# Group 0's block products piled up in PSUM, and a second group wholly on two levels, in a routed low-rank FFN kernel

## The chip, the cores and the metric

The kernel runs on one core of a Trainium2 chip. A core has a matrix engine (TensorE, PE in the profile, with its weight loads as PEld), a vector engine (VectorE, DVE), a scalar engine (ScalarE, ACT), GpSimd (POOL) and SyncE (SP), which here only issues DMAs. They run side by side and meet at semaphores. Matmuls write to PSUM, eight banks of 128 x 512 f32; the rest lives in SBUF. The metric is the device time of one execution in microseconds; lower is better. The kernel before takes 790.79 us, median of three runs (790.68 to 791.86).

## What is computed

All is f32. There are 64 samples of 64 channels and 1024 features, 4096 rows in all. Each sample picks one 64 x 64 matrix, which mixes its channels; the mixed rows z go through a low-rank layer of 64 adapters with rank 16, of which a router picks 16 per row; the result is added to x.

```python
W = weights[condition]                            # (64, 64, 64)
z = einsum('bct,bcd->bdt', x, W)                  # channel mix, per sample
scores = z @ Wr.T                                 # (4096, 64)
top_vals, top_idx = top_k(scores, 16)
G = zeros.at[rows, top_idx].set(softmax(top_vals))
h = einsum('nd,krd->nkr', z, A)                   # 1024 -> 64 * 16
out = einsum('nkr,kdr->nd', h * G[:, :, None], B) # 64 * 16 -> 1024
return x + 2 * out
```

The two large steps are products of 1024 x 1024 matrices (A, then B) with all rows.

## The kernel before

**Tiling.** Rows are handled in eight groups of 512. For a group, the first product ("h") is x A, 512 x 1024 by 1024 x 1024; mixing by W comes after it, since it acts on rows ("zp" matmuls, `gated`, L305), and VectorE multiplies the gates in on the way from PSUM to the tiles `hb`. The second product ("o") is `hb` times B, added to x and stored.

**Seven products instead of eight.** Each product is split into 2 x 2 quadrants and done by a Strassen-Winograd scheme: seven block products p1 to p7, called *parents*, of sums of quadrants of the left side (`left_sums`, L337: steps s1 to s4) and of the right side (`a_sums`, `b_sums`), and sums of their results. A parent on level 1 is a *whole* product: two halves of four matmuls of 512 columns. A parent on level 2 is split once more into seven *leaves* of two matmuls of 256 columns each, by the same scheme: `prepare` makes the left leaves on VectorE (tiles `l_t`), the right leaves are made once, staged in SBUF (`hs_...` for A, `os_...` for B), stored to DRAM and fetched again when used.

**The router** has 16 extra columns beside each 256 of A (272 in all, `KC`). From group 2 on the h parents carry them along, and `scores` finishes them with the channel mix. Groups 0 and 1 compute the router apart: `scores_t` (L170) multiplies x with `wr_sb`, `turn` transposes it back, and `scores` applies the mix. Then `route_top`, `exps`, `rest` (once for each of a group's four tiles), `scaled` and `gates` (transposes "gp" by TensorE, copied to `gg`) give the gates.

**Order of parents.** h of group 0, o of group 0, h of group 1, h of group 2, o of group 1, h of group 3, o of group 2, and so on. Group 0 is on level 1 throughout, and so are p1 and p2 of group 1's h; all else is on level 2. The order within a product is in `FIRST` (group 0) and `ORDER`.

**Who decides the order.** It is written out by hand. `run` (L544) issues a parent's instructions in program order for every engine, and hooks hang other work into it: `at(n, "mid" | "late" | "end", f)` runs f in the slot of parent n. Within a slot the left leaves of the next parent are prepared between "mid" and "late"; what is finished of the parent before is added up by its `done`. Each engine executes its own instructions in that order, and so does each DMA queue: nearly all DMAs are issued from SP, in order.

**Group 0's results.** Each whole parent has its own two banks. ScalarE copies them to an SBUF tile `m`, and `done` (L634 for h, L697 for o) adds such tiles to each other and to the output tiles `o`, wide adds of 128 x 1024 by VectorE.

**Leaf making.** `leaf_steps` (L392) gives for each right-hand block four VectorE steps and their stores; B's blocks without raw copies in the input also store their raw quadrants (L405, three DMAs). `a_steps` and `b_steps` are lists of such steps that hooks in group 0 work off. They stage in the pool `bsum` of four buffers, so a step waits for the store of the step that had its buffer. The leaves of A's p1 and p2 come last (staged in `zp`), in group 1's slots, since A11 and A21 are still used whole until then.

**Fetching.** `fetch` (L443) loads the next leaf in order of use into a ring of 13 buffers (`bp`); each level-2 product frees its buffer and fetches one. The first 13 fetches are hooked to the first two parents of group 1's h.

**Memory.** A's blocks stay. `bpool` holds B's blocks, `wr_sb` and helpers for group 0; `second_level` (L808) closes all of group 0's pools at once, at the start of group 1, and opens those of the second level in their room.

**The start.** x and A are loaded in the order of use from SP (the first x block from ScalarE's queue); ten warm-up matmuls run meanwhile. The row numbers `idx` for the gather of W come first on VectorE.

Of the kernel before, what the change touches and what calls it, by code (L numbers as in the profile page):

```python
# [24 lines left out]
RING = 13  # L25
# [4 lines left out]
def kernel(  # L30
# [47 lines left out]
    bpool = first_group.enter_context(tc.tile_pool(name="bpool", bufs=1, side="right"))  # L78
    mp0 = first_group.enter_context(tc.tile_pool(name="mp0", bufs=5, side="right"))
    rp0 = first_group.enter_context(tc.tile_pool(name="rp0", bufs=3, side="right"))  # L80
    bsum = first_group.enter_context(tc.tile_pool(name="bsum", bufs=4, side="right"))
# [10 lines left out]
    def load_x(g: int, i: int, j: int, queue=nc.sync):  # L92

        t = xq[g, i, j] = xp.tile([P, CH, HN], F32, tag=f"x{i}{j}", name=f"x_{g}_{i}{j}")
        queue.dma_start(t, x_t[g, i, j])
# [9 lines left out]
    load_x(0, 0, 0, nc.scalar)  # L105
    a11 = load_block("a11", a_t, 0, 0, apool, 2)
# [6 lines left out]
    wr_sb = bpool.tile([P, 2 * CH, K], F32, name="wr_sb")  # L113
# [4 lines left out]
    b11 = load_block("b11", b_t, 0, 0, bpool)  # L118
# [9 lines left out]
    for j in range(2):  # L128
        h = slice(j * C, (j + 1) * C)
        nc.vector.tensor_scalar(  # L130
            idx[h],
            cond_b[h].rearrange("p (n j) -> p n j", j=2)[:, :, j],
            float(C),
            row[h],
            ALU.mult,
            ALU.add,
        )
# [4 lines left out]
    for _ in range(10):  # L142
        nc.tensor.matmul(idle, lhsT=ident, rhs=ident, start=True, stop=True)
    two_i = bpool.tile([P, K], F32, name="two_i")
# [15 lines left out]

    gather(0)
# [8 lines left out]
    def scores_t(st):  # L170
# [14 lines left out]
        st_sb = bpool.tile([P, 2 * HN], F32, tag="st_sb", name=f"st_sb_{g}")  # L185
# [3 lines left out]
    def turn(st):  # L189
# [7 lines left out]
        zr = bpool.tile([P, TPG, K], F32, tag="zr", name=f"zr_{g}")  # L197
# [194 lines left out]
    def leaf_steps(k, j, block, pool, tag="leaf"):  # L392

        (q11, q12), (q21, q22) = quads(block, WIDTH[k])
        made = {}

        def staged(name):
            if tag == "z":
                return pool.tile([P, 2, 2 * (HALF + KC)], F32, tag=tag, name=name)[:, :, : WIDTH[k]]
            t = pool.tile([P, 2 * (HALF + KC)], F32, tag=tag, name=name)  # L400
            return t[:, : 2 * WIDTH[k]].rearrange("p (c k) -> p c k", c=2)
# [5 lines left out]
        def step(op_, p, a, b):  # L407
            def f():
                made[p] = staged(f"{k}s_{j}_{p}")
                op_(made[p], *(made[v] if isinstance(v, str) else v for v in (a, b)))  # L410
                nc.sync.dma_start(leaf_d[k, j, p], made[p])
# [3 lines left out]
        if k == "o":  # L415
# [8 lines left out]
        return [  # L424
            step(sub, "p7", q22, q12),
            lambda: sub(q12, q12, q11),
            step(sub, "p6", q22, q12),
            step(sub, "p4", q21, "p6"),
        ]


    parents, to_fetch, ring, stay = [], [], [], {}
# [10 lines left out]
    def fetch():  # L443
        if to_fetch:
            key = to_fetch.pop(0)
            t = pools["bp"].tile([P, 2 * (HALF + KC)], F32, tag="b", name="l{}_{}_{}".format(*key))
# [12 lines left out]
    pools = {"mp": mp0, "rp": rp0}  # L459

    def parent(kind, st, j, level, left, whole, done):


        g = st["g"]
        par = {"kind": kind, "g": g, "j": j, "level": level, "done": done}

        width = WIDTH[kind] if g > 1 else HALF

        def begin():
            name = f"m_{g}_{kind}_{j}"  # L470
            if g and kind == "h":
                m = pools["zp"].tile([P, 2, 2 * (HALF + KC)], F32, tag="z", name=name)
            else:
                m = pools["mp"].tile([P, 2, BANK], F32, tag="m", name=name)
            v = halves(m)[:, :, :, :width]
            par.update(m=m, v=v, q=[[v[:, i, k, :] for k in range(2)] for i in range(2)])
            par.update(bank={}, val={}, width=width)

        def whole_w(c):
            w = whole[j][:, c, :]  # L480
            return w.rearrange("p (d k) -> p d k", d=2)[:, :, :HALF] if kind == "h" else w

        def half(s):

            par["bank"][s] = acc.tile([P, BANK], F32, tag="acc", name=f"{kind}_{g}_{j}_{s}")
            for c in range(CH):
                piece(s, c)
# [499 lines left out]
```

## Time and profile before

| what | value |
|---|---|
| median of three runs | 790.79 us (790.68 to 791.86) |
| the profiled execution's own time | 790.09 us |
| its span, first to last instruction | 788.0 us |
| TensorE busy | 774.4 us, 98% of the span |
| VectorE busy | 626.8 us, 80% |
| ScalarE busy | 191.7 us, 24% |
| DMA moved | 206.82 MB, mean 262 GB/s |
| group 0's h begins on TensorE | 6.16 us |
| group 0's o begins | 61.81 us |
| group 1's h begins | 120.72 us |
| group 2's h begins | 166.37 us |
| last matmuls begin | 779.64 us |

The profile is one execution. Busy times are unions per engine; the difference between the execution's time and its span is outside the instructions. In rows of the timeline the columns are start, length, engine, line, operation, output tiles and input tiles, shape, count, and in brackets the idle time of the engine before it and what ended it. A matmul in f32 appears as two records. Names in the profile have no numbers: `h_p_x` is a bank of some parent of h, `o_p_w` of o, `hs_p_p` and `os_p_p` are staged leaves, `h_p_p` and `o_p_p` their places in DRAM, `lh_p_p` and `lo_p_p` the fetched ones, `a`, `at`, `b`, `bt` the right-hand blocks.

### The profile page before, as it was taken

Reading aid. Unit: us, or ns where it says so; the run is one execution under the profiler, and the core shown is the slowest. Engines: PE = TensorE matmul, PEld = TensorE weight load, DVE = VectorE, ACT = ScalarE, POOL = GpSimd, SP = SyncE. Lnnn points to the kernel's source line nnn. Section 1 sums busy time; section 2 is a strip of 40 time slices with the busy share of each in tenths; the row PEclk is TensorE's granted clock in tenths of the full one; section 3 lists DMA queues with packets and bytes.
Section 4 is the critical chain, followed back from the end, with each engine's and each line's share of the span. In section 5 each row is a group of like instructions: output and inputs, shape, how many; then the busy total and the mean of one; then the engine's idle time right before and its main releaser. Section 6 shows DMA issues by size and latency. Waiting matters only on the chain.

```text
span 788.0 us, 14615 instructions
## 1 busy us (share of the span) xinstructions
PE 774.4 (98%) x5348; PEld 608.9 (77%) x5348; DVE 626.8 (80%) x1297; ACT 191.7 (24%) x500; POOL 36.8 (5%) x39
## 2 busy tenths in 40 slices
PE   9999999999999999999999999999999999999996
PEld 5444445888888888887888888888888888887885
DVE  0789798878688868897788976888868887788886
ACT  1131121321222222222222222232223232222221
POOL 4100100002000020000200010000200000000000
PEclk9999999999999999999999999999999999999998
DMA  8813779955888858896788958889488894688895
GB/s 319 335 58 140 258 280 374 334 170 150 323 271 286 294 197 294 277 305 226 257 270 283 315 184 304 249 280 353 124 313 280 275 340 142 201 271 281 304 366 215
DMA packets 114454, 206.82 MB, mean 262 GB/s; under 512 B 12112, under 2 KB 32848, under 8 KB 113488
## 3 DMA queue, kind: packets, MB, share of 16 engines
q1 hardware_dynamic: 112928, 204.02, 76.1%
q0 software_dynamic: 1024, 1.05, 0.5%
q8 instruction: 43, 0.70, 0.4%
q10 hardware_dynamic: 432, 0.82, 0.3%
q14 instruction: 27, 0.22, 0.1%
HBM read 172.74 MB, written 33.11 MB: 261 GB/s over the span
## 4 chain that ended last, share of the span: by engine, by line
PE 83%; DVE 9%; DMA 6%; issue 1%; SPq 0%; ACT 0%; DVEq 0%
PE h_p_x L530 21%; PE o_p_x L530 19%; PE h_p_w L530 11%; PE o_p_w L530 10%; PE h_p_y L530 5%; PE h_p L495 5%; PE o_p_y L530 5%; PE zp L318 4%; DMA h_p_p<-hs_p_p 2%; DVE o L84 2%; DVE os_p_p L87 2%; DMA o_p_p<-os_p_p 1%; PE gp L298 1%; DMA out_dram<-o 1%; DVE hs_p_p L87 1%
## 5 line engine op out<-in xcount | busy, mean ns | idle before, releaser
L530 PE MATMUL o_p_x<-lo_p_p,l_t 128*128 128x256 f32 x584 | 143.0, 379 | 0.8 <-issue 0.8
L530 PEld LDWEIGHTS o_p_x<-lo_p_p,l_t 128*128 128x128 f32 x584 | 110.8, 190 | 16.6 <-issue 1.2
L84 DVE TENSOR_TENSOR o<-o,m_o_p 128x1024 f32<-128x1024 f32 (+1 forms) x73 | 86.0, 1196 | 1.2 <-DMA o<-in_x_dram 0.7
L84 DVE TENSOR_TENSOR m_h_p<-m_h_p,m_h_p 128x1088 f32<-128x1088 f32 (+1 forms) x56 | 70.3, 1267 | 5.5 <-ACT m_h_p L492 5.2
L84 DVE TENSOR_TENSOR m_h_p<-h_p_w,l_a 128x272 f32<-128x272 f32 (+1 forms) x47 | 20.6, 438 | 57.1 <-PE h_p_w L530 57.0
L153 POOL DMA_INDIRECT w_st<-in_cw_dram,idx x32 | 36.0, 1125 | 530.4 <-PE zp L318 513.9
L530 PE MATMUL h_p_x<-a,l_t 128*128 128x272 f32 (+1 forms) x208 | 55.9, 391 | 0.0
L530 PE MATMUL h_p_w<-lh_p_p,l_t 128*128 128x272 f32 (+1 forms) x188 | 51.2, 395 | 0.0
L530 PE MATMUL o_p_w<-lo_p_p,l_t 128*128 128x256 f32 x196 | 51.0, 383 | 0.0
L530 PE MATMUL h_p_x<-lh_p_p,l_t 128*128 128x272 f32 (+1 forms) x188 | 50.5, 391 | 0.0
L564 ACT COPY l_b<-h_p_x 128x272 f32<-128x272 f32 (+1 forms) x47 | 18.1, 385 | 118.8 <-PE h_p_x L530 118.8
L530 PEld LDWEIGHTS h_p_x<-a,l_t 128*128 128x128 f32 x208 | 39.5, 190 | 7.8
L331 DVE TENSOR_TENSOR hb<-zp,gg 128x512 f32<-128x512 f32 x64 | 39.9, 683 | 7.0 <-PE zp L318 7.0
L530 PE MATMUL h_p_x<-at,l_t 128*128 128x272 f32 (+1 forms) x168 | 45.0, 390 | 0.0
L564 ACT COPY l_b<-o_p_x 128x256 f32<-128x256 f32 x49 | 18.3, 373 | 103.7 <-PE o_p_x L530 103.7
L530 PEld LDWEIGHTS h_p_x<-lh_p_p,l_t 128*128 128x128 f32 x188 | 35.7, 190 | 6.9
L530 PEld LDWEIGHTS o_p_w<-lo_p_p,l_t 128*128 128x128 f32 x196 | 36.6, 190 | 5.1
L530 PEld LDWEIGHTS h_p_w<-lh_p_p,l_t 128*128 128x128 f32 x188 | 35.0, 191 | 6.5
L84 DVE TENSOR_TENSOR m_o_p<-o_p_w,l_a 128x256 f32<-128x256 f32 x48 | 20.3, 423 | 24.3 <-PE o_p_w L530 24.3
L318 PEld LDWEIGHTS zp<-w_st,m_h_p 64*64 64x64 f32 x2048 | 31.7, 135 | 7.8 <-issue 6.9
L530 PEld LDWEIGHTS h_p_x<-at,l_t 128*128 128x128 f32 x168 | 31.9, 190 | 6.3
L318 PE MATMUL zp<-w_st,m_h_p 64*64 64x64 f32 x2048 | 34.3, 220 | 0.3 <-issue 0.3
(148 smaller groups left out, 1342.6 us busy)
## 6 DMA issues: line engine op xcount, KB each, us to landing
lo_p_p<-o_p_p SPq DMA_DIRECT2D x280, 256.0 KB
lh_p_p<-h_p_p SPq DMA_DIRECT2D x141, 272.0 KB
o<-in_x_dram SPq DMA_DIRECT2D x32, 512.0 KB
lo_p_p<-in_b_t_dram SPq DMA_DIRECT2D x63, 256.0 KB
x<-in_x_t_dram SPq DMA_DIRECT2D x31, 512.0 KB
out_dram<-o SPq DMA_DIRECT2D x31, 512.0 KB
o_p_p<-os_p_p SPq DMA_DIRECT2D x28, 256.0 KB
h_p_p<-hs_p_p SPq DMA_DIRECT2D x21, 272.0 KB
```

Source lines behind the costliest of these rows:

```text
L84: nc.vector.tensor_tensor(o, a, b, ALU.add)
L87: nc.vector.tensor_tensor(o, a, b, ALU.subtract)
L153: nc.gpsimd.indirect_dma_start(out=w_st[:, i, :], out_offset=None, in_=cw, in_offset=bass.IndirectOffsetOnAxis(ap=idx[:, n : n + 1], axis=0),)
L298: nc.tensor.transpose(gp[:, i, :], st["g2"][i].rearrange("p a k -> p (a k)"), ident)
L318: nc.tensor.matmul(zp[b][e * D : (e + 1) * D, c, s, :], lhsT=halves(z)[r, s, c // 2, ds(c % 2 * P + e * D, D)], rhs=ws[g][r, 2 * i + s, :] ...
L331: nc.vector.tensor_tensor(tokens(hb[j, i])[:, :, :, b, :], zp[b], g_ij[:, :, :, b, :], ALU.mult)
L495: nc.tensor.matmul(par["bank"][s], lhsT=left()[j][:, c, ts(s, P)], rhs=whole_w(c), start=c == 0, stop=c == CH - 1, skip_group_check=True,)
L530: nc.tensor.matmul(bank, lhsT=v[:, c, :], rhs=w[:, c, :width], start=first and c == 0, stop=c == 1, skip_group_check=True,)
L564: nc.scalar.copy(par["val"][n], par["bank"]["x"])
```

## The change

**Whole products pile up.** In group 0 the parents of one product no longer have banks of their own. Three pairs of banks, X, Y and W, take them in turn, and a parent that belongs to a sum is accumulated on what its pair holds. For h the pair X takes p1, then p6, p7 and p4 on top; W takes p5 and then p3; Y takes p2. ScalarE copies X where a partial sum is itself needed (after p1, p6, p7 and p4 for h, after p1, p6 and p5 for o); VectorE adds the other pairs from PSUM, one bank at a time (`add_piled`).

**Group 1.** All its h parents are on level 2 and carry the router's columns, as in the later groups. Its `scores_t` and `turn` go; its scores, routing, gates and `gated` move into the slots of group 2's h, in a schedule that the last group shares with one slot's difference. In the last group the fourth `rest`, `scaled` and `gates` each come a place earlier.

**Leaves.** A's p1 and p2 leaves are made at the very start, before all sums, by four steps each. As A11 and A21 are still needed whole, the partial difference goes to a tile apart, and ScalarE copies it into the block later. Their six stores are issued on ScalarE's queue. The index computation and group 0's gather come after the first four of these steps, group 0's x sums before `a_sums(1)`. B's leaves come in another order and partly earlier, A's others too; `b_sums(4)` is one slot earlier.

**Pools.** Blocks that are done with early (`b11`, `bt3`, `wr_sb` and helpers) go to `epool`, closed after o's fifth parent; there the first six ring buffers (`bp0`) and the pools for left leaves and copies are opened, and the first six fetches are hooked to the slot of o's sixth parent. The rest of the pools is closed and reopened at group 1, as before.

**Loads.** The first x block comes in two parts, A11 in four; there are seven warm-up matmuls. The output tiles' input quarters are loaded in the order (0,0), (1,1), (1,0), (0,1), in the last group at o's parents -2, -1, 1 and 2.

```diff
-RING = 13
+RING, RING0 = 13, 6
...
-    load_x(0, 0, 0, nc.scalar)
-    a11 = load_block("a11", a_t, 0, 0, apool, 2)
+    load_x(0, 0, 0, nc.scalar, 2)
+    a11 = load_block("a11", a_t, 0, 0, apool, 4)
...
-    for _ in range(10):
+    for _ in range(7):
         nc.tensor.matmul(idle, lhsT=ident, rhs=ident, start=True, stop=True)
...
-    def leaf_steps(k, j, block, pool, tag="leaf"):
+    def leaf_steps(k, j, block, apart=None):
...
+        queue = nc.sync if apart is None else nc.scalar
...
-                nc.sync.dma_start(leaf_d[k, j, p], made[p])
+                queue.dma_start(leaf_d[k, j, p], made[p])
...
+        t1 = q12 if apart is None else apart.rearrange("p (c k) -> p c k", c=2)
+        steps = [
             step(sub, "p7", q22, q12),
-            lambda: sub(q12, q12, q11),
-            step(sub, "p6", q22, q12),
+            lambda: sub(t1, q12, q11),
+            step(sub, "p6", q22, t1),
             step(sub, "p4", q21, "p6"),
         ]
+        return steps if apart is None else steps + [lambda: nc.scalar.copy(q12, t1)]
...
+            pool = pools["bp0" if fetched[0] % RING < RING0 else "bp1"]
...
-        width = WIDTH[kind] if g > 1 else HALF
+        width = WIDTH[kind]
...
+    PILES = {
+        "h": dict(p1="X", p2="Y", p5="W", p6="x", p7="x", p4="x", p3="w"),
+        "o": dict(p1="X", p7="W", p6="x", p2="Y", p5="x", p4="w", p3="x"),
+    }
+
+    def whole_parent(kind, st, j, left, whole, piles, done, copied=None):
+        n = PILES[kind][j].lower()
...
+        def piece(s, c):
...
+            nc.tensor.matmul(
+                piles[n, s],
+                lhsT=left()[j][:, c, ts(s, P)],
+                rhs=w,
+                start=c == 0 and PILES[kind][j].isupper(),
+                stop=c == CH - 1,
+                skip_group_check=True,
+            )
...
+    def add_piled(o, piles, n):
+        for s in range(2):
+            add(o[:, s, :], o[:, s, :], piles[n, s])
...
-        f for j in ("p2", "p1", "p3", "p5", "p6", "p7", "p4") for f in leaf_steps("o", j, br[j], bsum)
+        f for j in ("p1", "p2", "p7", "p3", "p5", "p6", "p4") for f in leaf_steps("o", j, br[j])
...
+    def second_level():
+        open_pools(early, ("lp", 2), ("lt", 2), ("bp0", RING0), side="right")
+
+    def steady():
+        open_pools(first_group, ("mp", 3), ("zp", 6), ("bp1", RING - RING0), ("rp", 4))
...
+    steps_of(first_steps["p1"], 4)
+    rows_to_gather()
+    gather(0)
+    steps_of(first_steps["p2"], 4)
     x_operands(st)
+    sums(st, "x_sums", "s1_s2")
     a_sums(1)
-    sums(st, "x_sums", "s1_s2")
     a_sums(2)
...
-    at(o + 4, "mid", b_sums, 4)
...
+    at(o + 3, "end", b_sums, 4)
+    for k, lst, n in (
+        (h + 2, b_steps, 4),
+        (h + 3, b_steps, 4),
+        (h + 5, a_steps, 4),
+        (h + 6, a_steps, 5),
+        (o, a_steps, 2),
+        (o + 1, b_steps, 5),
+        (o + 1, a_steps, 1),
+        (o + 2, a_steps, 6),
+        (o + 3, a_steps, 2),
+        (o + 4, b_steps, 7),
+        (o + 5, b_steps, 7),
+    ):
+        at(k, "end", steps_of, lst, n)
+    at(o + 6, "mid", steps_of, b_steps, 2)
     at(o + 6, "end", steps_of, b_steps, 99)
...
-    at(o + 2, "mid", scores_t, nxt)
-    at(o + 3, "mid", turn, nxt)
...
+    at(o + 4, "end", second_level)
+    at(o + 5, "mid", fetches, 3)
+    at(o + 5, "end", fetches, 3)
+    h = sts[1]["h"]
+    at(h + 0, "mid", fetches, 4)
+    at(h + 0, "end", fetches, 3)
...
+    for st in sts[1:]:
+        n, g = st["h"] + 7, st["g"]
+        near = g in (1, NG - 1)
...
+        if near:
+            slots = ((2, "end"), (3, "late"), (3, "end"), (4, "late"))
...
+        at(n + (4 if near else 8), "end" if near else "mid", scaled, st)
+        at(n + (5 if near else 8), "mid" if near else "late", gates, st)
```

## The prediction

> **What bounds the kernel now.** I read the page's busy shares first, then TensorE's list of waits, then the timelines of TensorE, VectorE and SP over the first 180 us (where the change lies), and busy time by stretches for the DMA rate.
>
> ```profile
> PE 774.4 (98%) x5348; PEld 608.9 (77%) x5348; DVE 626.8 (80%) x1297; ACT 191.7 (24%) x500; POOL 36.8 (5%) x39
> ...
> PE idle L143 <- POOL ident masks.py:199: 1.5, 1, 1.5
> PE gp L298 <- ACT g L286: 1.4, 1, 1.4
> ...
> PE o_p L495 <- DVE b L87: 0.8, 1, 0.8
> PE h_p_w L530 <- DVE m_h_p L84: 0.5, 1, 0.5
> PE o_p L495 <- DVE hb L87: 0.4, 1, 0.4
> ```
> TensorE works 774.4 of 788.0 us. Less TensorE work shortens the span one for one, every new TensorE wait lengthens it one for one, and removing waits can give only the few us listed. VectorE counts where it makes TensorE late.
>
> ```profile
> 20.34 3.67 PE L177 MATMUL st<-x,wr_sb 128*64 128x256 f32 x32
> 23.94 3.70 PE L495 MATMUL h_p<-a,sum_p 128*128 128x512 f32 x8
> ...
> 120.72 13.90 PE L495 MATMUL h_p<-a,x 128*128 128x512 f32 x32
> 134.45 1.03 PE L530 MATMUL h_p_x<-at,x 128*128 128x256 f32 x4
> ...
> 140.49 1.03 PE L530 MATMUL h_p_x<-at,l_t 128*128 128x256 f32 x4
> ```
> Differences of starts are the true costs, since matmuls overlap: 3.60 us for the router's scores, 13.73 for two whole products, 6.04 for a two-level product of 256 columns (seven leaves). One of 272 columns takes 6.41 (chain of waits, 287.40 to 293.81).
>
> ```profile
> 0.00:5.00 5.00, 3.47 (x16) 3.47 (x17) 0.29 (x2) 1.28 (x1) 0.77 (x7) 1.00 0.61 206
> 5.00:10.00 5.00, 4.60 (x15) 2.39 (x15) 0.44 (x2) 0.00 (x0) 0.00 (x0) 1.00 0.84 297
> 10.00:20.00 10.00, 10.00 (x24) 4.10 (x22) 1.27 (x3) 1.76 (x3) 7.54 (x8) 1.00 1.05 390
> ...
> 120.00:130.00 10.00, 10.00 (x25) 4.42 (x24) 7.95 (x24) 1.66 (x3) 0.00 (x0) 1.00 1.07 399
> ```
> The last two columns are DMA share and GB/s: DMA is full from 10 us on, and again at 120 to 130. It is the second resource without slack.
>
> ```profile
> 18.99 2.43 DVE L87 TENSOR_TENSOR a<-a,a 128x2176 f32<-128x2176 f32 x1 [8.70 <-DMA a<-in_a_t_dram]
> ...
> 85.09 1.42 DVE L87 TENSOR_TENSOR os_p_p<-b,os_p_p 128x512 f32<-128x512 f32 x2 [4.47 <-DMA h_p_p<-hs_p_p]
> ...
> 122.40 0.69 DVE L87 TENSOR_TENSOR os_p_p<-b 128x512 f32<-128x512 f32 x1 [1.55 <-DMA o_p_p<-os_p_p]
> ...
> 129.89 0.42 DVE L84 TENSOR_TENSOR l_t<-x 128x256 f32<-128x256 f32 x1
> ...
> 74.98 1.84 SPq L95 DMA_DIRECT2D x<-in_x_t_dram  x4
> ```
> Leaves are staged in four buffers, so VectorE stops until a store four leaves back has landed (the waits at 85.09 and 122.40), and what is queued behind the leaf stops too. Group 1's first left-hand leaves (`l_t`) come at 129.89; they are needed only after two whole products, from 134.45.
>
> **TensorE's work.** Group 1: before 13.73 + 5 x 6.04 = 43.93; after 7 x 6.41 = 44.87: +0.94. Its `scores_t` goes: -3.61 (83.38 to 86.99). `turn`: -0.84 (93.96 to 94.80). Its scores become 32 small matmuls, 1.07 us (694.63 in the chain), instead of 16 in 0.61: +0.46. Group 0 issues the same matmuls. Sum -3.05.
>
> **Waits that go.** `b_sums(4)` is a slot earlier: -0.76. The hidden sums wait (0.41): between the product and the next stand the same zp and one subtraction, but fewer adds lie ahead on VectorE: -0.41. The wait at 142.88 belonged to late A leaves, which are now made first: -0.50. The last group's fourth `rest` moves ahead of about 2.7 us of adds (716.74 to 719.46), its gate transposes do not move on TensorE: -1.42. Sum -3.1; with the work, -6.1.
>
> **The adds.** Piles take some 7 us of adds from VectorE in group 0, at 1.2 us each (74.46 row: 1.22). Adding a bank pair from PSUM is two 128x512 operations, by the row `hb<-zp` 0.64 each, so as dear as one wide add. The copies by ScalarE fall too. All of this is beside TensorE: 0, unless VectorE binds.
>
> **The start.** x and A11 in smaller parts let the first product begin near 4.6 instead of 6.16 (seven warm-up pairs at 4.23/10 us end at 4.5). But the second needs A21. Bytes ahead of it: 3.31 MB; the windows give 2.52 MB by 10 us, then 390 GB/s: 12.0, plus about 1.2 to land, and the trace begins that product at 13.30. Gain 0 (bounds -0.3 to +0.5).
> The eight A-leaf subtractions (8 x 0.73 = 5.9 us) lie in VectorE's idle 10.3 to 19; without that cover they would cost their length. Group 0's gather goes behind four of them, to about 13: four issues (3.8 us) and 9.1 to landing make 26, before the scores at 32. ScalarE's queue now has six stores that wait for VectorE ahead of its first copy; the copy is not due until the next pile write, after 30.
> The stores are not free. They are 6 x 0.279 = 1.67 MB, 4.1 us at 404 GB/s (20 to 30 us), put among the loads. By the same sum A12 is complete at 17.6 and seen by VectorE at 18.99, so the router's weights (5.73 MB) land near 19.7, only just before `st` at 20.34. Shares: the first x block (ScalarE's queue) and half of A11 (SP's), alike in size and pieces, landed at 6.12 and 5.94, so equal shares; that puts all stores ahead of the weights: +4.1. The Trainium skill (DMA: Bandwidth & Descriptors, Queues, rings and completion order) says an engine takes turns between queues by packets; against loads in pieces of 8704 bytes, stores in 2176 get less than half and about four fifths of them come before the weights: 3.3. `st` then starts 2.7 to 3.5 late: **+3.1** (bounds 0 to 4.1). What follows (`p5`, `p6`) has its sums by then.
>
> **The entry to group 1.** Two whole products used to cover it; now the third leaf product of its first parent needs `t2`, 1.8 us in. Group 1 starts at 120.72 - 5.06 (scores, turn, sw) - 1.17 + 3.1 = 117.6, so `t2` is due at 119.4. VectorE's order puts the four `l_t` behind `os_p4_p5`, whose buffer is that of `os_p6_p5`.
> (1) Group 0's o starts at 64.9; its second zp block ends 9.4 later, as before (61.81, 71.22): 74.3. hb, sum, two A7 steps (1.29 + 1.22 + 0.72 + 0.72): 78.2. Group 1's x loads go out behind that store.
> (2) From x issue to the landing of the first store behind it took 10.1 (74.98 to 85.09). Now three raw copies and a leaf lie there, 0.77 MB more: 2.2. VectorE, out of buffers, resumes at 78.6 + 12.3 = 90.9.
> (3) Up to the first output store: two leaves 1.43, `o` 1.3, sum 1.2, A4 2.9, A3 1.45, `o` 1.2, sum 1.15, b21 2.25, A3 1.45, `o` 1.3 = 15.6: 106.5. Product p4, which needs b21 (103.8), is due at 103.7: no matter.
> (4) From that store to `os_p6_p5`: nine leaves and six raw copies of 0.262 MB, three fetches of 0.279, two stores and a load of 0.524: 6.34 MB in one queue, in order. At 399 GB/s 15.9 us; at 364 (stretches with many raw copies) 17.4. First data 1.2 after issue, landing 0.5 after the last: 124.1 to 125.6.
> (5) `os_p4_p5` 0.70, t1 and t2 0.8: 125.6 to 127.1, against 119.4. TensorE waits 6.2 to 7.7: **+7.0** (bounds 3, x loads at the rate of other loads, to 8.5). Next late would be the following parent's `l_t`; they come with their product. SP's fetches for it, issued behind the same stores, land some 3 us ahead of use.
>
> **Edits with one answer.** The last group's input quarters are loaded in another order and later on SP: each still has a product (6 us) before its add, against 4.55 for such a load (113.05); 0, and without that cover the add waits, not TensorE. The ring's split, the pools' sides and the earlier B leaves issue what was issued before; six A-leaf stores leave SP's queue at 135 to 146, where six fetches for group 1's first two products take their room. New waits on reused memory concern stores of a product or more earlier: 0.
>
> **The clock.** The trace's warm-up matmuls take 0.21 us each and the same shape at 49.94 takes 0.11: half rate after the idle start. No later idle stretch here passes 1.5 us, so the rows alone price a long wait at its length. The Trainium skill (TensorE: Matmul & The Clock Gate, Part 1) lets the array fall to half rate after an idle window of about 3.4 us and stay for as long: 3.4/2 = 1.7 more for the 7 us wait, nothing for 3.1. With the rule the sum has +1.7; I take it.
>
> **Sum.** -6.1 + 3.1 + 7.0 + 1.7 = +5.7: span 793.7, its own execution 790.09 + 5.7 = 795.8. The median stands 0.70 above that execution: **796.5 us**.
>
> **Rivals.** *The entry does not bind* (faster): DMA empties as fast as VectorE fills it. For: VectorE alone would have the `l_t` about 111 (78.2, then 4.6 of adds and leaves, the 15.6 of (3), 12.5 of leaves and adds). Against: 4.47 us already lost at 85. It decides when `t2` comes by 119.4: 790.8 - 6.1 + 3.1 = 787.8. *The stores give way to the loads*: no wait at `st`, the entry as above: 793.4. *Neither*: 784.7. *VectorE becomes the bound in group 2's h*, where group 1's routing (0.8 + 4 x 1.2 us on VectorE) now lies: steady h products show VectorE 32.5 of 44.0 us, so there is room; if slots collide, 2 to 4 us on top: 799.5.
>
> **How the numbers follow.** Both waits 0.58 (own range 792.5 to 799); entry alone 0.12; `st` alone 0.14; neither 0.06; crowded group 2 0.10. The range reaches down to the third and up to the last: 787.5 to 800.5. Against 0.2% (1.6 us, what a measurement of this kernel can tell): slower 0.73, within 0.09 (small entry waits), faster 0.18.
>
> **What would show it.** TensorE `st` beginning at 23 to 24 behind a DMA wait; a wait of 6 to 8 us near 119 at `h_p_x` for `l_t`, VectorE's `os_p_p` then waiting for stores; no wait at the last `gp`. If the stores land fast or SP issues them earlier, the prediction is wrong on the low side.

## The result, and the profile after

The changed kernel takes 801.22 us, median of four runs (798.96 to 801.74), beside 790.73 us for the kernel before on the same chip (four runs, 789.72 to 791.86): a ratio of 1.0127, 95% interval 1.0103 to 1.0151. The forecast was 796.5 with a range of 787.5 to 800.5: the direction is right, but the time lies above the range, and the loss of 10.5 us is 1.8 times the 5.7 forecast. The profiled execution has a span of 799.7 us, 11.7 more than before.

First the page's head and TensorE's list of waits (what was waited for, us in total, times, longest). The 8.8 us at its top, ahead of the third leaf product of group 1's first parent, are called the entry wait below:

```profile
span 799.7 us, 14643 instructions
...
PE 773.6 (97%) x5342; PEld 612.2 (77%) x5342; DVE 623.9 (78%) x1310; ACT 184.1 (23%) x490; POOL 36.5 (5%) x39
...
PE h_p_x L505 <- issue: 8.8, 1, 8.8
PE st L183 <- DMA wr_sb<-in_wr_t_dram: 2.7, 1, 2.7
PE o_p_x L505 <- ACT l_r L598: 1.8, 1, 1.8
...
PE o_w L542 <- DVE b L90: 1.1, 1, 1.1
...
PE h_p_x L505 <- ACT l_r L598: 0.5, 1, 0.5
```

The last `gp` wait is gone, as forecast, and so are the two small ones. But the wait for B21 (`o_w`) has grown from 0.8 to 1.1 instead of going, and two waits for a ScalarE copy `l_r` are new, which the prediction did not have. `st` and the entry wait are the two it had.

The timeline of TensorE (start, length, engine, line, operation):

```profile
24.25 3.67 PE L183 MATMUL st<-x,wr_sb 128*64 128x256 f32 x32 [2.70 <-DMA wr_sb<-in_wr_t_dram]
...
119.91 1.08 PE L505 MATMUL h_p_y<-a,x 128*128 128x272 f32 x4
129.83 2.15 PE L505 MATMUL h_p_x<-lh_p_p,l_t 128*128 128x272 f32 x4 [8.84 <-issue]
131.78 2.02 PE L505 MATMUL h_p_w<-lh_p_p,l_t 128*128 128x272 f32 x4
133.59 2.02 PE L505 MATMUL h_p_x<-a,l_t 128*128 128x272 f32 x4
135.40 1.38 PE L505 MATMUL h_p_x<-a,x 128*128 128x272 f32 x4
136.62 1.08 PE L505 MATMUL h_p_y<-a,x 128*128 128x272 f32 x4
```

The trace names no releaser for the 8.84 us. VectorE's timeline does: the second `l_t` (t2) begins at 129.31 and ends at 129.73, 0.1 us before TensorE goes on, and ahead of it stand B leaves that wait for their buffers' stores:

```profile
92.55 0.69 DVE L90 TENSOR_TENSOR os_p_p<-bt 128x512 f32<-128x512 f32 x1 [9.06 <-DMA o_p_p<-os_p_p]
...
124.96 0.69 DVE L90 TENSOR_TENSOR os_p_p<-bt,os_p_p 128x512 f32<-128x512 f32 x1 [7.18 <-DMA o_p_p<-os_p_p]
...
128.25 0.69 DVE L90 TENSOR_TENSOR os_p_p<-b 128x512 f32<-128x512 f32 x1 [0.80 <-DMA o_p_p<-os_p_p]
128.85 0.42 DVE L87 TENSOR_TENSOR l_t<-x 128x256 f32<-128x256 f32 x1
129.31 0.42 DVE L90 TENSOR_TENSOR l_t<-l_t,x 128x256 f32<-128x256 f32 x1
```

The four products after the wait take 6.79 us (129.83 to 136.62) and not 4 x 0.917 = 3.67: another 3.1 us, at half rate. Starts of the same work in both traces split the 11.7 us:

| stretch on TensorE | before, us | after, us | difference | forecast |
|---|---|---|---|---|
| up to `st` | 20.34 | 24.25 | +3.9 | +3.1 |
| `st` to group 0's o | 41.47 | 41.47 | 0.0 | 0.0 |
| group 0's o to group 1's h | 58.91 | 53.27 | -5.6 | -6.2 |
| group 1's h to group 1's o | 92.68 | 107.01 | +14.3 | +10.2 |
| group 1's o to the end | 574.6 | 573.7 | -0.9 | -1.4 |
| sum | 788.0 | 799.7 | +11.7 | +5.7 |

(The forecast column is the prediction's own terms put where they fall: -6.2 is scores_t, turn, 16 small `sw` matmuls of 0.61, 0.76 and 0.41; +10.2 is 0.94 - 0.50 + 1.07 + 7.0 + 1.7.) The +14.3 is 8.84 of wait, 3.1 of half rate, 0.46 of `l_r`, 0.94 of wider products, 1.07 of group 1's `sw`, less 0.50; the 0.4 that is left is not assigned.

### The profile page after: what moved, and what is told of

Read it like the earlier page. It is cut to its first block, busy times and chain, and to the rows that moved or that the text cites. A ratio compares the mean times of both kernels' runs of the same rounds, so it can differ in the third digit from the quotient of the medians.

```text
span 799.7 us, 14643 instructions
## 1 busy us (share of the span) xinstructions
PE 773.6 (97%) x5342; PEld 612.2 (77%) x5342; DVE 623.9 (78%) x1310; ACT 184.1 (23%) x490; POOL 36.5 (5%) x39
## 4 chain that ended last, share of the span: by engine, by line
PE 89%; DMA 4%; DVE 4%; issue 2%; SPq 0%; ACT 0%; DVEq 0%; ACTq 0%
PE h_p_x L505 23%; PE o_p_x L505 20%; PE h_p_w L505 11%; PE o_p_w L505 10%; PE h_p_y L505 6%; PE o_p_y L505 5%; PE zp L324 4%; PE h_x L542 3%; DMA x<-in_x_t_dram 2%; PE h_w L542 2%; PE o_x L542 2%; PE o_w L542 1%; DVE o L87 1%; DMA o_p_p<-os_p_p 1%; DMA wr_sb<-in_wr_t_dram 1%
## 5 line engine op out<-in xcount | busy, mean ns | idle before, releaser
L87 DVE TENSOR_TENSOR o<-o,m_o_p 128x1024 f32<-128x1024 f32 (+1 forms) x67 | 78.7, 1193 | 0.5
L87 DVE TENSOR_TENSOR m_h_p<-h_p_w,l_a 128x272 f32<-128x272 f32 x49 | 21.5, 439 | 62.9 <-PE h_p_w L505 62.9
L505 PE MATMUL h_p_x<-lh_p_p,l_t 128*128 128x272 f32 x196 | 54.1, 399 | 9.3 <-issue 8.8
L87 DVE TENSOR_TENSOR m_h_p<-m_h_p,m_h_p 128x1088 f32<-128x1088 f32 x49 | 62.3, 1283 | 0.2
L505 PE MATMUL h_p_x<-a,l_t 128*128 128x272 f32 x224 | 61.4, 397 | 0.0
L505 PE MATMUL h_p_w<-lh_p_p,l_t 128*128 128x272 f32 x196 | 54.6, 402 | 0.0
L505 PEld LDWEIGHTS h_p_x<-a,l_t 128*128 128x128 f32 x224 | 43.1, 193 | 8.9
L598 ACT COPY l_b<-h_p_x 128x272 f32<-128x272 f32 x49 | 18.9, 385 | 121.9 <-PE h_p_x L505 121.9
L505 PE MATMUL h_p_x<-at,l_t 128*128 128x272 f32 x168 | 45.4, 392 | 0.0
L505 PEld LDWEIGHTS h_p_w<-lh_p_p,l_t 128*128 128x128 f32 x196 | 37.1, 194 | 7.3
```

The costliest lines, as they stand in the source:

```text
L87: nc.vector.tensor_tensor(o, a, b, ALU.add)
L505: nc.tensor.matmul(bank, lhsT=v[:, c, :], rhs=w[:, c, :width], start=first and c == 0, stop=c == 1, skip_group_check=True,)
L598: nc.scalar.copy(par["val"][n], par["bank"]["x"])
```

## The experiments

Edits are against the changed kernel, and from the ninth run on against the kernel of the eighth. Spans are of one profiled execution each; medians and intervals come from repeated runs beside the kernel before. e1 to e4, e5 to e8 and e9 to e11 were timed on three different chips, so it is the ratios that compare, not the medians. The ratios of e1, e2, e3 and e5 have intervals that overlap the changed kernel's (1.0103 to 1.0151), and e7's touches it: what is read from these rests on their traces.

### Is it the order on VectorE? (e1_sums_ahead)

```diff
-        if after and after["level"] == 2:
+        if after and after["level"] == 2 and "leaf" not in after:
...
-        (o + 5, b_steps, 7),
+        (o + 5, b_steps, 5),
...
-    at(o + 6, "mid", steps_of, b_steps, 2)
+    at(o + 6, "late", lambda: parents[sts[1]["h"] + 1]["prepare"]())
```

> The changed kernel, with VectorE's order altered at one place: the left-hand leaves of group 1's first two products are both made before the last six B leaves instead of behind one and between the others; no instruction is added or removed. Theory (the entry waits because l_t stands on VectorE behind a B leaf that waits for a staging buffer): the wait of 8.84 us before the third leaf product falls under 0.5, the products after it take 0.92 us each and not 1.8, and what is left moves to group 1's third product near 132, where the B leaves may still hold VectorE for up to 3 us; span 788 to 791. Rival (TensorE waits there for a B or A leaf fetched from DRAM): the wait stays at 8 to 9 us and the span at 799 to 800.

Measured: span 799.6; median 801.71, ratio 1.0136 (1.0109 to 1.0162). TensorE's timeline, then VectorE's:

```profile
127.41 1.08 PE L505 MATMUL h_p_x<-a,l_t 128*128 128x272 f32 x4
136.82 2.18 PE L505 MATMUL h_p_x<-lh_p_p,l_t 128*128 128x272 f32 x4 [8.33 <-ACT l_r L598]
```
```profile
134.65 0.69 DVE L90 TENSOR_TENSOR os_p_p<-b,os_p_p 128x512 f32<-128x512 f32 x1 [3.05 <-DMA o_p_p<-os_p_p]
135.26 0.68 DVE L90 TENSOR_TENSOR os_p_p<-b 128x512 f32<-128x512 f32 x1
135.86 0.43 DVE L87 TENSOR_TENSOR m_h_p<-h_p_y,l_r 128x272 f32<-128x272 f32 x1
```

The span holds 1.7 us of half rate at `st` by chance (see the last section), which the edit did not cause; from group 1's h to its o it takes 105.8 us against 107.0. The wait for `l_t` is gone, and the first product runs through; the second product then waits 8.33 us at the same place in its leaves. The adds of the first product's results stand on VectorE behind the last leaves, now until 135.86; they hold the one buffer of `l_r`, so that ScalarE's copy for the second product waits, and the matmul that writes on the copied bank waits for it. So neither theory held as put: here the order on VectorE decided which instruction was late and hardly how long. What has to be through before group 1 runs is the last leaf, and each leaf waits for a store. Whether stores are late by bytes or by something else is what the next runs ask.

### Is the half rate due to the idle stretch? (e2_kept_busy)

```diff
+        if par and par is parents[sts[1]["h"]]:
+            warm = acc.tile([P, P], F32, tag="acc", name="warm")
+            for _ in range(36):
+                nc.tensor.matmul(warm, lhsT=ident, rhs=ident, start=True, stop=True)
         if tail:
             third()
```

> The changed kernel, with 36 warm-up matmuls of 128x128 into a free bank put in TensorE's stream just ahead of the third leaf product of group 1's first parent, to fill most of its 8.84 us wait (36 x 0.22 = 7.9 us). Theory (the half rate of the following 5.5 us comes from the idle stretch itself): the same l_t time near 129.8, but the next four leaf products take 3.7 us and not 6.8, span lower by 3.1, about 796.6. Rival (the slow products come from something else at that time, such as loads that contend): span unchanged, 799 to 800.5.

Measured: span 797.3; median 799.69, ratio 1.0115 (1.0089 to 1.0141). TensorE's timeline:

```profile
120.89 8.20 PE L627 MATMUL warm<-ident 128*128 128x128 f32 x72
130.99 1.16 PE L505 MATMUL h_p_x<-lh_p_p,l_t 128*128 128x272 f32 x4 [1.89 <-issue]
131.98 1.08 PE L505 MATMUL h_p_w<-lh_p_p,l_t 128*128 128x272 f32 x4
...
134.73 1.08 PE L505 MATMUL h_p_y<-a,x 128*128 128x272 f32 x4
```

`l_t` came 1.2 us later in this execution (the leaf ahead of it waited 2.08 us and not 0.80), yet the four products take 3.74 us and not 6.79, while DMA moves as much as in the changed kernel (393 GB/s from 132.4 to 135.8). The half rate comes from the idle stretch: 3.1 us of the loss. All four executions agree: their mean granted clock is 0.995 to 0.998, where the changed kernel's four have 0.991 to 0.994. The ratio shows little of it; in the profiled execution `l_t` took 1.2 us of it back.

### What makes st late? (e3_weights_first, e4_leaves_later)

The first swaps two load issues:

```diff
-    a12 = load_block("a12", a_t, 0, 1, apool)
     wr_sb = epool.tile([P, 2 * CH, K], F32, name="wr_sb")
     nc.sync.dma_start(wr_sb, wr_t.rearrange("(c p) k -> p c k", p=P))
+    a12 = load_block("a12", a_t, 0, 1, apool)
```

> The changed kernel, with the router's weights loaded ahead of block A12 instead of behind it (two load issues swapped on SP's queue). Theory (st waits for those weights alone, and all of group 0 with its leaves moves up with it): st starts at 21.5 without a DMA wait; p5, whose operand VectorE ends at 25.9, then starts 0.0 to 0.8 late; the gain of 2.0 to 2.7 is kept through the entry: span 797.0 to 797.7. Rival (the leaf stores are bound by DMA from the start, so that the entry comes at the same time anyway): the wait at the entry grows by as much as st gains, span 799.5.

The second takes the stores out of the first loads' way:

```diff
-    steps_of(first_steps["p1"], 4)
...
-    steps_of(first_steps["p2"], 4)
...
-    for j in ("p1", "p2"):
-        at(h + 2, "end", steps_of, first_steps[j], 1)
+    for j, k in (("p1", 2), ("p2", 3)):
+        at(h + k, "end", steps_of, first_steps[j], 5)
```

> The changed kernel, with the A leaves of p1 and p2 made and stored two and three products later instead of at the very start, so that no store shares DMA with the first loads. Only the first 35 us are compared. Theory (the six stores delay the loads): the second product starts at 13.3 and not 14.4, st at 20.4 to 20.6 without a wait. Rival (the finer first loads do it): 14.4, and st still waits. Later VectorE has 5.9 us more to do before the gates and the B leaves, so the whole may come out between 796 and 806; no reading rests on that.

TensorE's timeline of e3, then of e4:

```profile
21.41 3.67 PE L183 MATMUL st<-x,wr_sb 128*64 128x256 f32 x32
26.48 3.70 PE L542 MATMUL h_w<-a,sum_p 128*128 128x512 f32 x8 [1.39 <-DVE a L90]
```
```profile
13.16 7.13 PE L542 MATMUL h_y<-a,x 128*128 128x512 f32 x16 [0.87 <-DMA a<-in_a_t_dram]
20.30 3.67 PE L183 MATMUL st<-x,wr_sb 128*64 128x256 f32 x32
```

With the stores away `st` starts at 20.30, as before the change (20.34), though the finer first loads stayed: the stores are its delay. Loading the weights first (e3) frees `st` as well, but A12 is then later by their bytes, and p5 waits 1.39 us for it and the gates another 0.38; group 0's o begins 0.2 us earlier (65.50 against 65.72) and group 1's h at the same 118.99. Span 798.5, median 799.03 (1.0101; 1.0078 to 1.0124). e3's question, whether the entry would move with the start, is not answered, as hardly any gain was left by then. e4 as a whole is slower (span 802.7, one run of 804.7). ScalarE issues the stores, and the last three of them wait for leaves that VectorE now makes at 44.5 to 47.4; ScalarE stands from 40.2 to 47.8 (7.54 us idle behind VectorE's leaf), and a copy that TensorE needs comes 3.43 us late:

```profile
49.91 6.65 PE L542 MATMUL h_x<-at,x 128*128 128x512 f32 x8 [3.43 <-ACT m_h_p L556]
```

The second product's own delay is not settled. It starts at 14.42 after the change, and at 13.16 in e4, which fits the stores; but two later kernels (e7 and e8 below) with the same instructions up to there start it at 13.18, and the others between 14.2 and 14.6. One execution's first loads differ by that much. `st` moves with them: with the router's weights behind A12 and the stores in place it starts between 22.75 and 24.51 in six profiles, 2.4 to 4.2 us later than before the change.

### The gates' place on ScalarE (e5_gates_behind_copy)

```diff
-        at(n + (4 if near else 8), "end" if near else "mid", scaled, st)
-        at(n + (5 if near else 8), "mid" if near else "late", gates, st)
+        at(n + (5 if near else 8), "mid", scaled, st)
+        at(n + (5 if near else 8), "late", gates, st)
```

> The changed kernel, with the four scalings of the gates in group 1 and the last group moved on ScalarE from the end of one product to the middle of the next (behind that product's first copy and its second), and the gate transposes from the middle to just behind them. Theory (the 1.83 us and 0.46 us at l_r are ScalarE's copies standing behind scalings that wait for VectorE's last rest): both waits go, no wait appears at gp, span 797.4. Rival (VectorE's rest is late for the gates in any case): the l_r waits go but gp waits 1 to 2 us in the last group, span 799 to 800.

ScalarE's timeline in the last group, of the changed kernel and then of e5:

```profile
731.72 1.28 ACT L292 ACTIVATE g<-es,invs 128x128 f32<-128x128 f32 x4 [2.42 <-DVE invs L286]
732.90 0.35 ACT L598 COPY l_r<-o_p_x 128x256 f32<-128x256 f32 x1
```
```profile
726.45 0.37 ACT L598 COPY l_r<-o_p_x 128x256 f32<-128x256 f32 x1 [0.49 <-PE o_p_x L505]
...
729.31 1.28 ACT L292 ACTIVATE g<-es,invs 128x128 f32<-128x128 f32 x4
731.01 0.59 ACT L305 COPY gg<-gp 128x512 f32<-128x512 f32 x1 [0.42 <-PE gp L304]
```

Above, the scalings wait for VectorE and `l_r` stands behind them, 4.2 us after the product that it copies began (728.73). Below, the copy goes first, the scalings find their operands ready, and nothing waits at `gp`. Both `l_r` waits are gone. Span 795.3, median 797.93 (1.0113; 1.0090 to 1.0137). Of the 4.4 us less in span the stretch from group 1's o to the end has 1.3 (572.4 against 573.7), 0.46 lie in group 2's h, and the rest is a start that happened to be 1.1 us earlier, smaller waits behind it and 1.0 us less at half rate at the entry, which are not due to the edit. The first theory holds.

### What makes the leaves late? (e6_x_early, e7_copies_early)

e6 moves group 1's x loads to where DMA is little used:

```diff
-        at(o, "end", load_x, 1, i, j)
+        at(h + 6, "end", load_x, 1, i, j)
```

> The changed kernel, with group 1's four x loads issued at the end of group 0's last hidden product (about 66 us, DMA little used) and not at the end of the first output product (79.6). Theory (the entry is the end of a chain that begins with B and A leaf stores behind those 2.1 MB): VectorE's wait of 9.06 us at 83 to 92 shrinks to 2 to 4, everything behind it on VectorE moves up 5 to 7 us, B21 is ready before its product (1.07 gone), the entry wait falls to 2 to 4 us; span 790 to 794. Rival (the stores and copies between 107 and 127 fill DMA whenever they begin, or wait for products): the 9.06 shrinks but the entry still waits 7 to 9 us, span 798 to 799.

e7 sends the unchanged quadrants as soon as their sums are made; `raws` holds what was the first step of p5, p6 and p7:

```diff
+            if j in ("p5", "p6", "p7"):
+                raws[j] = raw
+                return steps
             return steps if j in RAW else [raw] + steps
...
+    at(h + 4, "end", lambda: raws["p5"]())
+    at(h + 5, "end", lambda: raws["p6"]())
+    at(h + 6, "mid", lambda: raws["p7"]())
```

(The slots that held these steps take one step fewer.)

> The changed kernel, with the nine unchanged quadrants of B's sums (raw copies of p5, p6 and p7, 9 x 0.262 MB) sent to DRAM as soon as each sum is made (53 to 64 us, DMA little used) and not between the staged leaves. Theory (what the l_t wait for is the bytes ahead of a leaf store in SP's queue): 1.57 MB less ahead of the entry is 4.0 us at 390 GB/s and 0.79 MB less at 84 to 92 is 2.0 us; the entry wait falls to about 2.8 us, the wait for B21 goes, span 789.5 to 792.7. Rival (it is the number of staging buffers and the latency of each store, not bytes): entry wait 7 to 8.8, span 798 to 799.7.

VectorE's and TensorE's timelines of e6:

```profile
85.51 0.69 DVE L90 TENSOR_TENSOR os_p_p<-bt 128x512 f32<-128x512 f32 x1 [2.60 <-DMA o_p_p<-os_p_p]
...
118.76 0.69 DVE L90 TENSOR_TENSOR os_p_p<-bt,os_p_p 128x512 f32<-128x512 f32 x1 [7.13 <-DMA o_p_p<-os_p_p]
```
```profile
123.55 1.30 PE L505 MATMUL h_p_x<-lh_p_p,l_t 128*128 128x272 f32 x4 [4.48 <-issue]
```

| | changed kernel | e6 | e7 |
|---|---|---|---|
| VectorE's first wait, at 83 to 92 | 9.06 | 2.60 | 6.96 |
| TensorE's wait for B21 | 1.07 | none | none |
| entry wait | 8.84 | 4.48 | 5.29 |
| span | 799.7 | 792.3 | 794.2 |
| median | 801.22 | 796.15 | 796.57 |
| ratio to before, 95% | 1.0103 to 1.0151 | 1.0063 to 1.0094 | 1.0066 to 1.0104 |

Each takes some 4 us off the entry wait. e6 shows the chain: with 2.1 MB out of the queue at 80 us VectorE resumes 7.0 us earlier (85.51) and makes `l_t` 6.3 us earlier (122.57), though its second wait is as long as it was (7.13 against 7.18). TensorE, freed of the B21 wait and with an earlier start, is 1.9 us earlier too, so the wait falls by 4.4. e7 speaks for the bytes: VectorE resumes 1.9 us earlier (0.79 MB less, 2.0 expected) and makes `l_t` 4.7 us earlier (124.16), so that the 1.57 MB less ahead of the entry gave 2.8 us (4.0 expected). The second wait hardly shrinks in either (7.18 us, then 7.13 and 6.67): that bytes set its length too is argued and not shown, and no run gave the leaves more staging buffers. Both rivals, at 798 and more, fall; the expected entry waits were just too low for e6 and too low by 2.5 us for e7. e7's span holds 1.7 us that is not the edit's: its `st`, after a wait of 2.44 us, ran at half rate (5.29 us instead of 3.61 to the next product), which the longer wait of 2.70 us in the changed kernel did not bring.

### Together (e8_three_moves)

The edits of e3, e5, e6 and e7 in one kernel.

> The changed kernel with the x loads and the raw copies early, the gates' scalings behind the copy, and the router's weights ahead of A12 (the four edits run singly, together). Theory: entry wait, its half rate, the B21 wait and the l_r waits all gone, st's wait traded for a smaller one at p5: 799.7 - 1.1 - 8.8 - 3.1 - 2.3 - 0.5 = span 783.9, about 784.5 to 785.5 as a time, 0.7% under the kernel before. Rival (another limit stands just behind, such as VectorE's own work before the entry): a wait of 2 to 4 us stays at the entry, span 786 to 788.5.

Measured: span 786.1; median 787.86 of six runs (787.32 to 788.56), ratio 0.9970, 0.9958 to 0.9982: faster than the kernel before. TensorE's timeline and VectorE's:

```profile
119.40 1.16 PE L508 MATMUL h_p_x<-lh_p_p,l_t 128*128 128x272 f32 x4 [1.56 <-issue]
120.39 1.08 PE L508 MATMUL h_p_w<-lh_p_p,l_t 128*128 128x272 f32 x4
```
```profile
82.29 0.69 DVE L90 TENSOR_TENSOR os_p_p<-bt 128x512 f32<-128x512 f32 x1 [0.61 <-DMA o_p_p<-os_p_p]
...
115.41 0.69 DVE L90 TENSOR_TENSOR os_p_p<-bt,os_p_p 128x512 f32<-128x512 f32 x1 [6.45 <-DMA o_p_p<-os_p_p]
```

The entry waits 1.56 us, at full rate. VectorE's first wait is all but gone; the second still lasts 6.45 us, with an output store, three fetches and an input load of 0.5 MB ahead of the store that it waits for, but it now begins at 109 and no longer at 118. The span is 2.2 us over the expectation: 1.56 are this wait, 0.9 a new wait for a fetched leaf later on, and 0.3 come back elsewhere. So it ends where the rival put it (786 to 788.5), with a smaller wait than the rival's 2 to 4 us.

### Two edits on top (e9_p2_behind_a12, e10_first_sums_ahead, e11_all_six)

e9:

```diff
     gather(0)
-    steps_of(first_steps["p2"], 4)
     x_operands(st)
     sums(st, "x_sums", "s1_s2")
     a_sums(1)
+    steps_of(first_steps["p2"], 4)
     a_sums(2)
```

> The kernel of the four edits together, with p2's four A-leaf steps on VectorE moved behind the sums for p5 (x's sums and A12 - A11), so that the last three of the six early stores go out behind A12. Theory (p5's 1.47 us wait is A12 arriving behind those stores, and VectorE waiting for staging buffers): p5 waits under 0.4 us, span 784.7 to 785.3. Rival (A12's own load sets it): wait and span as they were, 786.

e10:

```diff
-        if after and after["level"] == 2:
+        if after and after["level"] == 2 and "leaf" not in after:
...
-        (o + 5, b_steps, 6),
...
+    at(o + 5, "end", steps_of, b_steps, 4)
+    at(o + 5, "end", x_operands, sts[1])
+    at(o + 5, "end", lambda: parents[sts[1]["h"]]["prepare"]())
+    at(o + 5, "end", steps_of, b_steps, 2)
...
-            at(h - 1, "mid", x_operands, st)
+            if g > 1:
+                at(h - 1, "mid", x_operands, st)
```

> The kernel of the four edits together, with the left-hand leaves of group 1's first product alone made ahead of the B leaf that waits 6.45 us for its buffer. Theory (with fewer bytes in the queue the leaves are through before the second product's left-hand leaves are due at 124): the last 1.56 us of the entry wait go and nothing takes its place, span 784.3 to 784.9. Rival (the wait moves to the second product, as it did without the early loads and copies): 1 to 2 us at the second product's first leaf operand, span 786.

e11 has both:

> The kernel of the four edits with both of these: if both theories hold, span 783.0 to 783.8 and a time of 784 to 785.5, 0.7% under the kernel before; if one falls, 784.5 to 785.5 in span.

| | e9 | e10 | e11 |
|---|---|---|---|
| span | 787.5 | 785.7 | 787.3 |
| median | 791.08 | 787.48 | 789.60 |
| ratio to before, 95% | 0.9995 to 1.0025 | 0.9949 to 0.9975 | 0.9972 to 0.9997 |

e9 loses, and neither theory had the reason. TensorE's timeline, then ScalarE's:

```profile
31.79 1.10 PE L200 MATMUL sp<-two_i,st_sb 128*128 128x64 f32 x8 [2.33 <-ACT st_sb L192]
```
```profile
11.40 17.45 ACTq L417 DMA_DIRECT2D h_p_p<-hs_p_p  x6
28.88 1.28 ACT L559 ACT_TABLE_LOAD   x1 [28.88 <-DVE hs_p_p L90]
```

p5's wait fell to 0.51 us, but the six stores are issued from ScalarE, in order, and the last is not due before VectorE has made its leaf. ScalarE stood there until 28.9 (in the changed kernel until 21.5), and the copy of `st` that `turn` needs came late.

The trace of e9 has only part of its loss: the profiled execution, 789.54 us, is among the three fastest of ten. The mean granted clock is 0.997 and 0.998 in two of the ten (789.01 and 789.54 us) and 0.993 to 0.996 in the other eight, four of which, at 0.993, took 792.25 to 793.05; all executions of e8 and e10 have 0.997 or 0.998. So in most executions of e9 TensorE ran some microseconds more at half rate. That they follow the wait of 2.33 us is likely, but no trace of such an execution was kept.

e10 does what was expected of it at the entry: no wait there, nor at the second product, where e1 had found it again; TensorE waits 0.48 us for a fetched leaf further on. The product that waited 1.56 us in e8 follows at once:

```profile
119.35 1.08 PE L508 MATMUL h_p_x<-lh_p_p,l_t 128*128 128x272 f32 x4
```

Its start in this execution was 1.1 us later than e8's with the same instructions there, and group 0's gates came 0.49 us late, so that its span gained only 0.4; from group 1's h to group 1's o it takes 95.75 us against 96.58. It is the fastest of all kernels run here, with a ratio of 0.9962 to the kernel before, though not measurably ahead of e8 (0.9970; the intervals overlap).

e11 has what both did: the wait of 2.33 us at `sp` as in e9, and in place of the entry wait 0.26 us a few leaf products later and 0.6 for a fetched leaf. As e9's theory fell, so did the sum expected of both; it missed the fallback (a span of 784.5 to 785.5) as well, and eight of its twelve executions show a mean clock of 0.995 or 0.996, as in e9.

## Why the prediction had the sign right and the size wrong

The span lost 11.7 us where the sum had 5.7. Four steps carry the 6.0 us between: the entry wait was 1.8 too small (8.84 for 7.0), the half rate behind it 1.4 (3.1 for 1.7), the wait for B21 grew by 0.3 where -0.76 was entered (1.1), and ScalarE's copies `l_r`, put at nothing, cost 2.3. `st` adds 0.8, and 1.4 come back in waits and gaps that no term had.

**Holds.** TensorE's work: group 0's o is 5.6 us shorter although the wait for B21 grew in it, and the wider products cost what the row of 272 columns said. The start's stores delay `st`, and group 1's entry is where the kernel loses. The chain named for it, x loads, stores behind them, leaves out of buffers, `l_t`, is the one that e6 and e7 shorten. No wait in TensorE's list is for a piling add.

**"`st` waits, +3.1": a size.** 3.9 measured (bound 4.1). The wait itself is 2.70; the rest is the second product's later start, put at 0. Of the two workings, equal shares (4.1) and turns by packets (3.3), the first is nearer in this profile, but over six profiles the delay is 2.4 to 4.2 us: this case does not tell the two apart, and that 3.1 came near is in part luck.

**"Product p4, which needs b21 (103.8), is due at 103.7: no matter", and the -0.76: wrong.** VectorE resumed at 92.55 and not at 90.9, B21 was done at 105.1, TensorE waited 1.07. This step had no slack, and a term that rests on 0.1 us of margin should have been entered with a cost. Entered was -0.76; the wait grew from 0.76 to 1.07: 1.1 us between forecast and result.

**"The entry to group 1, +7.0": a size, 8.84.** The x loads were issued at 79.55 where the working had 78.2 for the store ahead of them; from there the chain ran 1.2 to 1.7 us late, up to the output store at 107.7 (forecast 106.5); 0.8 of it is the start (group 0's o at 65.72, forecast 64.9). Step (4) let DMA drain at 364 to 399 GB/s. The rates in the stretches of 4 us from 108 to 128 were 335, 354, 307, 297 and 394, a mean of 337, and `l_t` came at 128.85 and not about 125.5. This is not one slower rate: in the first and the fourth of these stretches the DMA engines were busy for only 0.89 and 0.88 of the time, in the third they moved 307 GB/s while full. The working took a queue that is always full. TensorE too was later (118.99 for 117.6), which takes some of it back. Step (5) saw the lateness of `l_t` alone; e1 shows that the adds behind the leaves would have been just as late.

**"+1.7 for the clock": a size, 3.1.** The rule was read as one window at half rate, half of it lost. The granted clock (third column from the end) in stretches of 3.41 us of the changed kernel says otherwise:

```profile
122.36:125.77 3.41, 0.00 (x0) 0.00 (x0) 0.81 (x2) 0.00 (x0) 0.00 (x0) 1.00 1.05 392
125.77:129.18 3.41, 0.00 (x0) 0.00 (x0) 2.61 (x5) 0.00 (x0) 0.00 (x0) 0.50 1.06 402
129.18:132.60 3.42, 2.77 (x6) 2.19 (x7) 3.35 (x9) 0.39 (x1) 0.00 (x0) 0.50 1.03 378
132.60:136.01 3.41, 3.41 (x9) 2.51 (x8) 2.70 (x7) 0.36 (x1) 0.00 (x0) 0.50 1.08 393
136.01:139.42 3.41, 3.41 (x17) 2.82 (x16) 0.88 (x2) 0.80 (x3) 0.00 (x0) 1.00 1.06 400
```

In this trace the clock changes at ticks 3.41 us apart. After a stretch with no work at all (122.36 to 125.77) it is halved; the stretch that work fills from end to end (132.60 to 136.01) ends it; the one that work only partly fills does not. So the work from 129.83 to 136.01 ran at half rate, 6.2 us, half of them lost. The Trainium skill (TensorE: Matmul & The Clock Gate, Part 1) has this in the words that the window is free-running and that full rate comes after a busy one; the prediction used its length alone. Its condition for the fall, an idle window of about 3.4 us, is too strict for these runs: the last section shows half rate after stretches that held 0.91 and 1.36 us of work.

**"The last group's gate transposes do not move on TensorE: -1.42": wrong.** That looked only at who waited for the gates. The four scalings moved a slot ahead on ScalarE, past the copy `l_r`, and took with them their wait for VectorE's last `rest`; 1.83 us came back there and 0.46 in group 1, which shares the slots. The working named what is queued behind ScalarE's early stores, and not what is queued behind these scalings. e5 shows it by moving them back: no wait at `gp`, none at `l_r`. That the stretch from group 1's o to the end is 0.9 shorter all the same owes much to other things: two waits of 0.80 and 0.19 us went, and 0.5 us between the four transposes, which had followed the scalings one by one.

**Rivals.** The entry did bind, the stores did not give way, and no wait in group 2's h is due to VectorE's load; the only one there is the `l_r` of 0.46 us.

## What to carry to other kernels

When one engine stages data for another through a small ring of buffers, price the stage by the bytes that lie ahead of each store in the DMA queue, and send early what depends on nothing (here x loads and unchanged quadrants: from group 0's o to the fifth leaf product of group 1 TensorE takes 70.9 us in the changed kernel and 59.2 in e8). Reordering the engine's own instructions only picked another victim while the queue was full of bytes (e1), and took the rest of the wait away when it was not (e10). A moved instruction takes its wait along: list what stands behind it on its own engine, ScalarE included, and the DMAs that this engine issues. A wait of TensorE has two prices, its length, and the time at half rate that may follow, seen here after waits of 2.44 us and more.

## What the runs showed of the hardware that was not expected

- Behind these waits the half rate lasts whole multiples of one tick of 3.41 us: 10.24 us in the changed kernel (wait 8.84), 6.8 us in e7's entry (wait 5.29, from 123.10 to 129.93), 3.4 us in e6 (wait 4.48). It does not need an empty window. In e6 it began 0.9 us after work had resumed, and at `st` in e7 after a wait of only 2.44 us:

```profile
121.05:124.46 3.41, 0.91 (x4) 0.82 (x5) 2.66 (x7) 0.00 (x0) 0.00 (x0) 1.00 1.05 405
124.46:127.83 3.37, 3.37 (x10) 2.44 (x9) 3.33 (x7) 0.39 (x1) 0.00 (x0) 0.50 1.06 387
```
```profile
22.75 5.36 PE L183 MATMUL st<-x,wr_sb 128*64 128x256 f32 x32 [2.44 <-DMA wr_sb<-in_wr_t_dram]
28.04 3.70 PE L545 MATMUL h_w<-a,sum_p 128*128 128x512 f32 x8
```

  `st` takes 3.6 us at full rate, as after the wait of 2.70 us in the changed kernel, and 5.3 in e7 and after 2.75 us in e1. So a wait of 2.4 to 2.8 us may or may not cost 1.7 us more. The ticks fit as the reason: the stretch of 3.41 us ahead of the change held 1.36 us of work in e7 and 0.96 in e1, and in the changed kernel, with ticks counted back from 122.36, the stretch that ends at 23.38 held 1.58. This would be some of the spread between executions of one kernel. In the profiled executions the waits of 1.56, 1.89 and 2.33 us in e8, e2 and e9 were followed by full rate; for the last, the mean clocks of e9's other executions speak against a rule.
- The first loads differ between executions: the second product began between 13.18 and 14.62 us in nine profiles whose instructions up to there are the same. A conclusion on 1 us at the start needs more than one profile.
- A DMA issue that is not ready stops the engine that issues it: six stores kept ScalarE from its copies until 21.5 us in the changed kernel, where nothing waited for them, until 28.9 in e9, where it cost 2.33 us, and until 47.8 in e4, where it cost 3.43.
